# Projecting ten chunks of a second recurrence ahead of a stream of attention slots

## The chip, the core and the metric

The kernel runs on one core of one Trainium2 chip. The core has five engines with a queue of instructions each: TensorE (PE: matmuls, with weight loads as PEld), VectorE (DVE), ScalarE (ACT), GpSimd (POOL) and SyncE (SP, which issues the DMAs here). A queue is worked off in order; between engines, semaphores make one wait for another. The metric is the time of the launch in microseconds of the device, median of the runs shown, lower is better. All data is float32. In the trace each float32 matmul leaves two records, a transpose one.

## What is computed

Two batches of 4096 tokens with 256 channels go through two parts, each with a residual.

```python
x = x + attn(layernorm(x))   # a token-by-token recurrence over 4096 steps
x = x + ffn(layernorm(x))    # 2 layers of windowed attention and a gated MLP
# attn: xr, xk, xv mix each token with the one before it
r, k, v = xr @ W_r.T, xk @ W_k.T, xv @ W_v.T
# scan over tokens, for each channel:
p = max(b, k + u); out = (exp(b - p) * a + exp(k + u - p) * v) / (sum of both exps)
# ... a and b are updated; then
rwkv = sigmoid(r) * out
# group norm with mean and variance over all 4096 tokens of a batch, then @ W_o.T
# ffn, per layer: shift by a token, qkv, l2norm, rotary, 8 heads of 64,
#   attention over the own window of 128 tokens and the one before it, @ wo,
#   shift, layernorm, @ w1, a * gelu(g), @ w2
```

The group norm needs the whole batch before the first token of attention can start. So batch 0 has to finish its recurrence first; batch 1's recurrence can run beside the attention of batch 0.

## The kernel before: how it is tiled and ordered

The program is not written in the order in which it runs. Everything in `tile_block_kernel` goes through a `Plan`: each call on `nc.tensor`, `nc.vector` and so on is noted as an operation with its dependences, an estimated duration (`cost`) and a priority, the row set by `plan.at(row)` (lower goes first). `Plan.order` then places operations on the engines: on each engine, of those that can start first, the one of the lowest row. `give` emits them in that order (so nearly all instructions carry line 517). "Either" operations, mostly copies out of PSUM, go to ScalarE, or to VectorE where ScalarE is more than 700 ns (`LEAN`) later. A DMA is assumed to hold SP for 60 ns and to land 2000 ns or more after its issue. A group of matmuls into one bank, or what stands in a `piece()`, stays together.

The work, in rows:

- Rows from -101: recurrence one (`rec`, batch 0), in seven chunks of 512 tokens and two of 256. A chunk is loaded (`load`), normalized (`normed`), transposed so that channels lie on partitions (`transposed`) and projected to k, v, r (`project`, j = 1, 2, 0). Then `scans` runs the recurrence with scan instructions on VectorE and exponentials on ScalarE. Projection uses one of two ways. `split` multiplies the tokens and the shifted tokens by two scaled copies of the weights (`wnow` and `wold`): 24 matmuls of 512 columns in a chunk. `mixed` first mixes tokens and shifted tokens on VectorE (a difference `d`, then `xm` for each of k, v, r) and multiplies by the plain weights (`wraw`, which are loaded again over `wold`): half the matmuls.
- `group_norm` turns the statistics of the batch into a scale and a shift per channel.
- Slots n = 0 to 127 (rows 0 to 133, with a tail for the last blocks): one slot is one window of 128 tokens in one layer of one batch, and four slots make a block of 512 tokens. In a slot: q and k of the window are transposed (`transpose_qk`), `scores` multiplies them, `softmax` runs in four groups, `transpose_p` brings the probabilities back for `values`, and `kept`, `output` and `shift` finish the attention. Beside these, the slot projects q, k, v of the next window (`project(n + 1, j)`), squares, rotates and norms them, and runs a share of the MLP of the block before (`fill`: `gate`, `gelus`, `value`, `down`). `scores` is one piece: the values of the slot before, the last MLP rows (`down_ends`), then the eight score matmuls, in this order.
- `mixed_out` (layer 0 only) applies the group norm to a block (`z`), multiplies by W_o, adds x, stores the sum (`x1d`) and normalizes for attention; `transpose_x` transposes the block. Both take a block of 512 tokens as a whole.
- Recurrence two (`rec2`, batch 1) has 16 chunks of 256 tokens. Chunk 0 is projected ahead (row -0.5, `AHEAD` = 1), split. The scans of chunk c stand at slot 5 + int(c * 50 / 16), that is 5, 8, 11, ... up to 51, and chunk c + 1 is projected there, mixed.

```python
 for c in range(AHEAD):
        plan.at(-0.5)
        rec2.ahead(c, rec2.split)
...
            if NW + 1 + int(c * R_SLOTS / rec2.n) == n:
                plan.at(n + 0.5)
                if AHEAD <= c + 1 < rec2.n:
                    rec2.ahead(c + 1, rec2.mixed)
                rec2.scans(c)
```

Names in the profile: `arena` is the space that both recurrences share (their x, xT, k, v, r, factors and `wnow`); `bank` is any of the eight PSUM banks; `hm` holds the five 128-row parts of the MLP's hidden layer, which is free until the first block's MLP in slot 5; `kT`, `qT` are transposed keys and queries, `vr` the values shifted by a token and `dv` their difference, `pB` the probabilities for the older window, `tab` the rotary table, `h` the shifted input of the MLP, `zd` the recurrence's output in DRAM.

Of the kernel before, what the change touches and what calls it, by code (L numbers as in the profile page):

```python
# [15 lines left out]
P = 128  # L16
# [15 lines left out]
NEG = -1e38  # L32
MASKED = -3e38
R_SLOTS = 50
AHEAD = 1

ARENA = (
    (("m ls aa", 2 * T + 2, 1), ("wnow", 6 * D, 1), ("xT", 2 * T + 2, 2), ("x", 2 * T, 2), ("k v", 2 * T, 1)),
# [20 lines left out]
LEAN = 700  # L59
SLACK = 1.06  # L60
LOAD = 1283
TURN = {"row": 195, "col": 95, "full": 199}
SETS = {AF.Exp: 1, AF.Tanh: 1, AF.Gelu: 2, AF.Ln: 3}
QUADS = 4
# [2 lines left out]
class Place:  # L67


    def __init__(self, size, psum=False):  # L70
        self.size, self.psum = size, psum
        self.reads, self.writes = [], []
        self.real = None
        self.users, self.bank = set(), None
        self.turn, self.first = 0, None
# [101 lines left out]
class Plan:  # L177
# [38 lines left out]

    def dram(self, shape, name):
        place = Place(int(np.prod(shape[1:])))
        place.real = self.dram_pool.tile([P, place.size], F32, tag=name, name=name)
        return self.view(place, 0, shape)  # L220

# [75 lines left out]
    def cost(self, o):  # L297

        views = [*o.outs, *o.ins]
        n = max([v.idx.size for v in views] or [1])  # L300
        psum = any(v.place.psum for v in views)
        inside = sum(v.idx.size == n and not v.place.psum for v in o.ins)
        o.set, o.lock, o.half, o.passes, name, hold = None, False, "full", 0, o.name, None
        if o.eng == "tensor":
            trans = name == "transpose"
            left = o.args[1]
            move = o.args[2] if len(o.args) > 2 else o.args[1]
            cols = max(move.idx.size, left.idx.size) if not trans else P
            o.step = (1 if trans else 2) * (cols / 1.2 + (2 if cols >= 256 else 3))
            if not trans and left.shape[0] <= 64:  # L310
                o.half = "row"
            elif not trans and left.idx.size <= 64:
                o.half = "col"
            if o.half != "full":
                o.step /= 2
            o.time = o.step + 150
        elif o.eng == "vector":
            d = 150 + 1.04 * n
            if name == "tensor_tensor_reduce":
                d = 240 + 1.04 * n  # L320
            elif name == "tensor_tensor_scan":
                d, o.lock = 203 + 2.1 * n, True
            elif name == "scalar_tensor_tensor":
                d, o.lock = 200 + 1.05 * n, inside > 1
            elif name == "tensor_tensor":
                o.lock = inside > 1
            elif name == "tensor_scalar":
                d, o.lock = 155 + (1.27 if psum else 0.98) * n, not psum and n > 16
            elif name == "tensor_copy" and not psum:
                d, o.lock = 230 + 0.45 * n, n > 16  # L330
            elif name == "bn_aggr":
                d = 172
            elif name == "reciprocal":
                d = 147 + 4 * n
            o.step, o.time = max(d - 85, 60), d
        elif o.eng in ("scalar", "either"):
            d = (160 if psum else 195) + 0.83 * n
            if name == "scaled":
                d = 305 + 0.76 * n
            elif name == "activation":  # L340
                o.set = SETS.get(o.args[2])
                if o.args[2] == AF.Identity:
                    d = 365 + 0.87 * n
                elif isinstance(o.kw.get("bias"), View):
                    d += 85
            o.step, o.time = d - 100, d
            if "accum_out" in o.kw:
                o.time = d + 200
        elif o.eng == "gpsimd":
            o.lock = name != "memset"  # L350
            if name == "tensor_tensor":
                d = 430 + 156 * n if ALU.pow in o.args else 140 + 2.22 * n
            elif name == "tensor_scalar":
                d = 230 + 1.12 * n
            else:
                d = (100 if name == "memset" else 187) + 0.98 * n
            o.step, o.time = d, d
            hold = d if n > 64 else 100
        else:
            v = min(views, key=lambda v: v.shape[0] * v.idx.size)  # L360
            size = 4 * v.shape[0] * v.idx.size
            rows = max(v.shape[0] if v.shape[0] > 1 else v.shape[1] for v in views)
            ways = max(k for k in range(1, 17) if rows % k == 0)
            o.passes = size / 170 if ways == 16 else size / (25 * ways)
            o.step, o.time = 60, 2000 + o.passes
        o.hold = hold or o.time


    def order(self):
# [49 lines left out]
        while todo:  # L419
# [25 lines left out]
            for o in g:  # L445
# [21 lines left out]
                o.start = t  # L467
                if e == "sync":
                    dma = max(dma, t) + o.passes
                    o.end = max(t + time, dma + 2000)  # L470
                else:
                    o.end = t + time
                if o.lock and e in lock:
# [47 lines left out]
def kernel(ctx: ExitStack, tc: tile.TileContext, a: dict, out: bass.AP):  # L521
# [62 lines left out]
    class Recurrence:  # L584


        def __init__(self, b, lengths, most, spots):
            self.b, self.most, self.spots = b, most, spots
            self.turns = {}
            self.len = lengths  # L590
            self.off = [sum(lengths[:c]) for c in range(len(lengths))]
            self.n = len(lengths)
# [73 lines left out]
        def mixed(self, c, j):  # L666

            ch, tr = self.chunks[c], self.len[c]
            if "d" not in ch:
                d = ch["d"] = self.t("d", tr)  # L670
                nc.vector.tensor_tensor(d, ch["xT"][:, :, 1:], ch["xT"][:, :, :tr], ALU.subtract)
            xm = self.t("xm", tr)
            for i in range(2):
                nc.vector.scalar_tensor_tensor(
                    xm[:, i, :],
                    ch["d"][:, i, :],
                    vec[:, j, i : i + 1],
                    ch["xT"][:, i, :tr],
                    ALU.mult,
                    ALU.add,  # L680
                )
            return [(wraw, xm[:, i, :], i) for i in range(2)]
# [7 lines left out]
                for wt, off in ((wnow, 1), (wold, 0))  # L690
            ]

        def project(self, c, j, how):

            ch, tr = self.chunks[c], self.len[c]
            parts = how(c, j)
            dst = ch[j] = self.t("rkv"[j], tr)
            per = T // tr
            for o0 in range(0, 2, per):
                pm = bank([P, T])  # L700
# [13 lines left out]
                else:  # L714
                    nc.scalar.activation(to, of, AF.Tanh, scale=0.5)

        def ahead(self, c, how):
            row = plan.row
            plan.at(row - 1)
            self.load(c)  # L720
# [1 line left out]
            self.transposed(c)  # L722
            plan.at(row)
            for j in (1, 2, 0):
                self.project(c, j, how)


        def factors(self, y, c):
# [156 lines left out]
    def mixed_out(k):  # L885
# [2 lines left out]
        if l:  # L888
            return
        x, z, g = xs[k], zs[k], groups[b]  # L890
        for h in range(2):
            nc.scalar.activation(
                z[:, h, :], z[:, h, :], AF.Identity, bias=g[:, 1, h : h + 1], scale=g[:, 0, h : h + 1]
            )
        for w0 in range(0, NW, 2):
            py = bank([P, 2, D])
            for w in range(2):
                for h in range(2):
                    nc.tensor.matmul(
                        py[:, w, :],  # L900
                        z[:, h, (w0 + w) * P : (w0 + w + 1) * P],
                        wot[:, h, :],
                        start=(h == 0),
                        stop=(h == 1),
                    )
            nc.vector.tensor_tensor(x[:, w0 : w0 + 2, :], x[:, w0 : w0 + 2, :], py, ALU.add)
        nc.sync.dma_start(out=x1d[b][c], in_=x)
        for w in range(NW):
            normed(x[:, w, :])

    def normed(x):

        st = tile_of([P, 6], "st", 4)
        mv = tile_of([P, 2], "mv", 6)
        nc.vector.bn_stats(st, x)
        nc.vector.bn_aggr(mv, st)
        rs = tile_of([P, 1], "rs", 6)
        rsqrt_of(rs, mv[:, 1:2], 1, LN_EPS, ALU.add)
        nc.vector.tensor_scalar(x, x, mv[:, 0:1], rs, ALU.subtract, ALU.mult)

    def transpose_x(k):

# [4 lines left out]
            nc.gpsimd.memset(xT[:, 1, 0:1], 0.0)  # L927
        else:
            nc.gpsimd.tensor_copy(xT[:, 1, 0:1], xTs[k - 1][:, 1, T : T + 1])
        for i in range(2):  # L930
            pt = bank([P, T])
            for w in range(NW):
# [116 lines left out]
    def scores(n):  # L1049
# [6 lines left out]
        ks = slice(me, me + 1) if lone(n) else slice(me - 1, me + 1)  # L1056
        sims[n] = [bank([P, 2, 2 * W]) for _ in range(4)]
        with piece():
            if n:
                values(n - 1)  # L1060
            down_ends(n)
            for hp in range(HEADS // 2):
                for r in range(2):
# [5 lines left out]
                        start=True,  # L1069
                        stop=True,  # L1070
                    )

    def softmax(n, g):

# [255 lines left out]
        for t, n in (("pB", 1), ("h", 2), ("hT", 1), ("sq", 1), ("t2", 1), ("qk", 2), ("x", 4))  # L1330
        for i in range(n)
    ]
    lent = [(p, 0) for p in lent] + [(plan.places["hm_0"], i * 2 * T) for i in range((NM - 1) // 2)]
    spots = [{}, {}]
    for b, parts in enumerate(ARENA):
        o = 0
# [6 lines left out]
    for t in "kvrfgeq":  # L1343
        while len(spots[0].setdefault(t, [])) < 2:
            spots[0][t].insert(0, lent.pop())

    plan.at(-101)
    rec = Recurrence(0, [T] * (NB - 1) + [T // 2] * 2, T, spots[0])
# [14 lines left out]
    for j in (1, 2, 0):  # L1363
        rec.project(0, j, rec.split)
    rec2 = Recurrence(1, [TR] * (S // TR), TR, spots[1])
    for c in range(rec.n):
        if c + 1 < rec.n:
            plan.at(-90 + c)
# [8 lines left out]
        plan.hold = None  # L1377
    rec.group_norm()
    for c in range(AHEAD):
        plan.at(-0.5)  # L1380
        rec2.ahead(c, rec2.split)
    plan.at(-0.5)
    nc.sync.dma_start(out=wraw, in_=a["w_rkv"])
    rec2.start()
    plan.at(-1)
    nc.gpsimd.memset(ends, 1.0)
# [13 lines left out]
    for n in range(NN + 6):  # L1400
# [5 lines left out]
        for c in range(rec2.n):  # L1406
            if NW + 1 + int(c * R_SLOTS / rec2.n) == n:
                plan.at(n + 0.5)
                if AHEAD <= c + 1 < rec2.n:
                    rec2.ahead(c + 1, rec2.mixed)  # L1410
                rec2.scans(c)
                if c + 1 == rec2.n:
                    rec2.group_norm()
# [142 lines left out]
```

## Time and profile before

| what | value |
|---|---|
| median of 3 runs | 3010.59 us (3009.65 to 3012.26) |
| the profiled execution | 3013.12 us |
| its span on the core | 3011.2 us, 48808 instructions |
| DMA | 182.50 MB, mean 61 GB/s |
| DMAs issued by SP | 1496 |
| of the chain that ended last | PE 80%, DVE 9%, ACT 5%, DMA 2% |

Columns of the views: in the page's slices each digit is the busy share of a fortieth of the span in tenths (one slice is 75.3 us), and PEclk is the clock that TensorE was granted. A timeline row has start, length, engine, line, operation, output and inputs with shapes, the number of merged instructions, and in brackets the idle time of the engine before it with what ended it. A group row has the shape, the count, then busy us and mean ns of one, then the idle time before such instructions and who ended it. The end of a matmul is modelled, and so its start-to-start distance says more than its length.

### The profile page before, as it was taken

Reading aid. Unit: us, or ns where it says so; the run is one execution under the profiler, and the core shown is the slowest. Engines: PE = TensorE matmul, PEld = TensorE weight load, DVE = VectorE, ACT = ScalarE, POOL = GpSimd, SP = SyncE. Lnnn points to the kernel's source line nnn. Section 1 sums busy time; section 2 is a strip of 40 time slices with the busy share of each in tenths; the row PEclk is TensorE's granted clock in tenths of the full one; section 3 lists DMA queues with packets and bytes.
Section 4 is the critical chain, followed back from the end, with each engine's and each line's share of the span. In section 5 each row is a group of like instructions: output and inputs, shape, how many; then the busy total and the mean of one; then the engine's idle time right before and its main releaser. Section 6 shows DMA issues by size and latency. Waiting matters only on the chain.

```text
span 3011.2 us, 48808 instructions
## 1 busy us (share of the span) xinstructions
PE 2947.5 (98%) x15500; PEld 1912.2 (64%) x15500; DVE 2218.2 (74%) x5077; ACT 2024.9 (67%) x5378; POOL 1437.8 (48%) x1705
## 2 busy tenths in 40 slices
PE   9978999999999999999999999999999999999998
PEld 4456566666666666666666666666666666666665
DVE  7888877888788888787676766667766666667663
ACT  7877786777767777676666566656666666666663
POOL 2226655445445454555544544545444545555550
PEclk9989999999999999999999999999999999999999
DMA  2322112111112121111122221111112121111110
GB/s 83 114 74 95 40 54 64 57 56 54 61 57 69 63 63 59 51 56 53 51 63 81 85 60 59 61 61 60 46 47 75 56 63 57 55 55 54 46 43 24
DMA packets 178314, 182.50 MB, mean 61 GB/s; under 512 B 27044, under 2 KB 147716, under 8 KB 177544
## 3 DMA queue, kind: packets, MB, share of 16 engines
q1 hardware_dynamic: 178056, 179.38, 19.4%
q8 instruction: 123, 2.02, 0.3%
q14 instruction: 135, 1.11, 0.1%
HBM read 79.17 MB, written 33.55 MB: 37 GB/s over the span
## 4 chain that ended last, share of the span: by engine, by line
PE 80%; DVE 9%; ACT 5%; DMA 2%; issue 1%; SPq 1%; POOL 1%; DVEq 0%; POOLq 0%; ACTq 0%
PE bank L517 80%; DVE arena L517 3%; SPq L517 1%; ACT arena L517 1%; DMA h<-x 1%; DVE bank L517 1%; ACT pr L517 1%; ACT L517 1%; DVE nmx L517 1%; DVE sq L517 1%; ACT pr L513 1%; DVE x L517 1%; DVE rn L517 0%; DVE qk L517 0%; DVE pB L517 0%
## 5 line engine op out<-in xcount | busy, mean ns | idle before, releaser
L517 PE MATMUL bank<-wqkv,xT 128*128 128x512 f32 x1536 | 722.0, 597 | 0.4 <-ACT xT L517 0.2
L517 POOL TENSOR_TENSOR t<-qk,tab 128x256 f32<-128x256 f32 x512 | 395.3, 792 | 527.2 <-ACT qk L517 408.1
L517 PE MATMUL bank<-hT,w 128*128 128x512 f32 (+1 forms) x1408 | 644.7, 594 | 0.0
L517 ACT ACTIVATE pr<-bank,nmx 128x129 f32<-128x129 f32 (+1 forms) x1024 | 364.6, 376 | 164.8 <-DVE nmx L517 158.3
L517 PEld LDWEIGHTS bank<-hT,w 128*128 128x128 f32 (+1 forms) x1408 | 258.9, 189 | 269.0 <-issue 247.6
L517 PEld LDWEIGHTS bank<-wqkv,xT 128*128 128x128 f32 x1536 | 268.0, 191 | 229.2 <-issue 219.2
L517 POOL TENSOR_TENSOR rn<-rn,mhalf 128x16 f32<-128x16 f32 x128 | 387.8, 3030 | 8.8
L513 ACT ACTIVATE pr<-pr,sums 128x129 f32<-128x129 f32 (+1 forms) x1004 | 329.4, 413 | 42.7 <-DVE pr L517 41.3
L517 DVE TENSOR_REDUCE rn<-sq 128x16 f32<-128x1024 f32 x128 | 155.6, 1215 | 209.6 <-ACT sq L517 209.6
L517 DVE COPY_PREDICATED bank<-packs,bank 128x254 f32<-128x254 int32 x496 | 186.0, 420 | 151.1 <-PE bank L517 150.7
L517 PE MATMUL bank<-w,hm 128*128 128x256 f32 x1280 | 287.3, 379 | 0.0
L517 PEld LDWEIGHTS bank<-w,hm 128*128 128x128 f32 x1280 | 241.4, 190 | 33.2 <-issue 1.3
L517 PE MATMUL bank<-wo,oT 128*128 128x256 f32 x1024 | 250.3, 387 | 0.0
L517 PE MATMUL bank<-kT,qT 64*128 64x256 f32 (+1 forms) x2048 | 246.1, 380 | 0.0
L517 PEld LDWEIGHTS bank<-wo,oT 128*128 128x128 f32 x1024 | 187.9, 190 | 68.3 <-issue 41.0
L517 ACT COPY qk<-bank 128x512 f32<-128x512 f32 x217 | 126.8, 585 | 151.5 <-PE bank L517 143.8
L517 POOL TENSOR_TENSOR dv<-vr,vt 128x512 f32<-128x512 f32 x124 | 168.7, 1360 | 124.5 <-PE bank L517 108.7
L517 PEld LDWEIGHTS bank<-mats,pr 128*128 128x128 f32 x1148 | 134.0, 135 | 136.7 <-issue 54.0
L517 ACT ACTIVATION_READ_ACCUMULATOR pr<-bank,nmx 128x1 f32 x1024 | 218.6, 214 | 0.0
L517 DVE TENSOR_TENSOR pB<-bank,backs 128x512 f32<-128x512 f32 x248 | 169.7, 684 | 66.4 <-PE bank L517 45.6
L517 PEld LDWEIGHTS bank<-kT,qT 64*128 64x128 f32 x2048 | 190.5, 187 | 31.4 <-issue 6.5
L517 POOL TENSOR_TENSOR tab<-tab,qks 128x256 f32<-128x256 f32 x128 | 119.2, 932 | 183.3 <-DMA tab<-in_c_rot_dram 166.2
(150 smaller groups left out, 5573.8 us busy)
## 6 DMA issues: line engine op xcount, KB each, us to landing
vr<-vt SPq DMA_DIRECT2D x124, 224.0 KB
tab<-in_c_rot_dram SPq DMA_DIRECT2D x128, 128.0 KB
kT<-kT SPq DMA_DIRECT2D x64, 256.0 KB
z<-zd SPq DMA_DIRECT2D x16, 512.0 KB
x<-in_x_dram SPq DMA_DIRECT2D x16, 512.0 KB
x1d<-x SPq DMA_DIRECT2D x16, 512.0 KB
x<-x1d SPq DMA_DIRECT2D x16, 512.0 KB
h<-x SPq DMA_DIRECT2D x128, 64.0 KB
```

Of the source, the lines that this page charges most:

```text
L513: self.nc.scalar.activation(dst, src, AF.Copy, scale=scale)
L517: getattr(getattr(self.nc, o.eng), name)(*args, **kw)
```

## The change

Five edits:

1. `AHEAD` goes from 1 to 10, so chunks 0 to 9 of recurrence two are projected in one place, with their loads at row 3 and their projections at row 4. `SPLIT` = 3 of them are split, the others mixed, with the weights loaded again between (row -0.5). `INSIDE` = 2 of them leave k, v, r in the arena. The eight others put them into one of three `far` buffers, from which SP stores them to DRAM (`away`); `back` loads them at the slot where they were projected before. Early chunks have a `d` and an `xm` buffer of their own. These five buffers lie in `hm`. In exchange recurrence one no longer borrows space in `hm`, and the turns of xT, x, k, v, r start at the other buffer.
2. For block 0 alone, `mixed_out` and `transpose_x` go by 128 tokens: z, W_o, sum and normalization of each 128 tokens stand by themselves, the normalized tokens go into another x tile, and each 128 tokens have a transpose bank and an eviction of their own.
3. The planner's costs: a DMA holds SP for 370 ns (580 or 800 for one between two SBUF tiles, by how it divides) instead of 60, and it lands after 2500 ns (`LAND`) instead of 2000.
4. In `scores`, the values of the slot before come after the score matmuls instead of ahead of them.
5. `normed` can write to another tile than it reads.

```diff
-AHEAD = 1
+AHEAD = 10
+SPLIT = 3
+INSIDE = 2
...
+            inner = len(views) == 2 and not any(v.place.outer for v in views)
+            o.step = 370 if not inner else 580 if ways in (1, 16) else 800
+            o.time = LAND + o.passes
...
             for j in (1, 2, 0):
-                self.project(c, j, how)
+                self.project(c, j, how, ("far", "far", "far") if away else "rkv")
+                if away:
+                    d = self.away[c, j] = plan.dram([P, 2, self.len[c]], f"away_{c}_{j}")
+                    nc.sync.dma_start(out=d, in_=self.chunks[c][j])
+
+        def back(self, c):
+            for j in (1, 2, 0):
+                dst = self.chunks[c][j] = self.t("rkv"[j], self.len[c])
+                nc.sync.dma_start(out=dst, in_=self.away[c, j])
...
+        if k == 0:
+            xs[k] = tile_of([P, NW, D], "x", 4)
+        for w0 in range(0, NW, 1 if k == 0 else 2):
+            ws = range(w0, w0 + (1 if k == 0 else 2))
+            if k == 0 or w0 == 0:
+                cols = slice(w0 * P, (w0 + 1) * P if k == 0 else T)
...
+            if k == 0:
+                normed(xs[k][:, w0, :], x[:, w0, :])
...
+        if k == 0:
+            for w in range(NW):
+                pt = bank([P, 2, P])
+                for i in range(2):
+                    nc.tensor.transpose(pt[:, i, :], x[:, w, i * P : (i + 1) * P], ident)
+                either(xT[:, :, 1 + w * P : 1 + (w + 1) * P], pt)
+            return
...
         with piece():
-            if n:
-                values(n - 1)
             down_ends(n)
...
+            if n:
+                values(n - 1)
...
+    spare = [(plan.places["hm_0"], i * 2 * TR) for i in range(NM - 1)]
+    spots[1].update(earlyd=spare[:1], earlyxm=spare[1:2], far=spare[2:])
...
     for c in range(AHEAD):
-        plan.at(-0.5)
-        rec2.ahead(c, rec2.split)
+        if c == SPLIT:
+            plan.at(-0.5)
+            nc.sync.dma_start(out=wraw, in_=a["w_rkv"])
+        plan.at(4)
+        rec2.chunks[c]["early"] = True
+        rec2.ahead(c, rec2.split if c < SPLIT else rec2.mixed, c >= INSIDE)
...
                 if AHEAD <= c + 1 < rec2.n:
                     rec2.ahead(c + 1, rec2.mixed)
+                elif INSIDE <= c + 1 < AHEAD:
+                    rec2.back(c + 1)
                 rec2.scans(c)
```

More of the change, by code (lines that the diff above doesn't have):

```diff
@@ L61 @@
 LOAD = 1283
+LAND = 2500
 TURN = {"row": 195, "col": 95, "full": 199}
@@ L72, in __init__ @@
         self.reads, self.writes = [], []
+        self.outer = False
         self.real = None
@@ L218, in dram @@
         place = Place(int(np.prod(shape[1:])))
+        place.outer = True
         place.real = self.dram_pool.tile([P, place.size], F32, tag=name, name=name)
@@ L364, in cost @@
             o.passes = size / 170 if ways == 16 else size / (25 * ways)
-            o.step, o.time = 60, 2000 + o.passes
+            inner = len(views) == 2 and not any(v.place.outer for v in views)
+            o.step = 370 if not inner else 580 if ways in (1, 16) else 800
+            o.time = LAND + o.passes
         o.hold = hold or o.time
@@ L469, in order @@
                     dma = max(dma, t) + o.passes
-                    o.end = max(t + time, dma + 2000)
+                    o.end = max(t + time, dma + LAND)
                 else:
@@ L588, in __init__ @@
             self.b, self.most, self.spots = b, most, spots
-            self.turns = {}
+            self.turns, self.away = {}, {}
             self.len = lengths
@@ L668, in mixed @@
             ch, tr = self.chunks[c], self.len[c]
+            early = "early" if ch.get("early") else ""
             if "d" not in ch:
-                d = ch["d"] = self.t("d", tr)
+                d = ch["d"] = self.t(early + "d", tr)
                 nc.vector.tensor_tensor(d, ch["xT"][:, :, 1:], ch["xT"][:, :, :tr], ALU.subtract)
-            xm = self.t("xm", tr)
+            xm = self.t(early + "xm", tr)
             for i in range(2):
@@ L691, in split, with project @@
             ]
-        def project(self, c, j, how):
+        def project(self, c, j, how, put="rkv"):
             ch, tr = self.chunks[c], self.len[c]
             parts = how(c, j)
-            dst = ch[j] = self.t("rkv"[j], tr)
+            dst = ch[j] = self.t(put[j], tr)
             per = T // tr
@@ L715, in project, with ahead @@
                     nc.scalar.activation(to, of, AF.Tanh, scale=0.5)
-        def ahead(self, c, how):
+        def ahead(self, c, how, away=False):
             row = plan.row
@@ L890, in mixed_out @@
         x, z, g = xs[k], zs[k], groups[b]
[L891 to L897, printed above, removed]
+        if k == 0:
[4 more added lines that the diff above has]
+                cols = slice(w0 * P, (w0 + 1) * P if k == 0 else T)
+                for h in range(2):
+                    nc.scalar.activation(
+                        z[:, h, cols],
+                        z[:, h, cols],
+                        AF.Identity,
+                        bias=g[:, 1, h : h + 1],
+                        scale=g[:, 0, h : h + 1],
+                    )
+            py = bank([P, len(ws), D])
+            for w in ws:
                 for h in range(2):
                     nc.tensor.matmul(
-                        py[:, w, :],
-                        z[:, h, (w0 + w) * P : (w0 + w + 1) * P],
+                        py[:, w - w0, :],
+                        z[:, h, w * P : (w + 1) * P],
                         wot[:, h, :],
@@ L905, in mixed_out, with normed @@
                     )
-            nc.vector.tensor_tensor(x[:, w0 : w0 + 2, :], x[:, w0 : w0 + 2, :], py, ALU.add)
+            x1 = x[:, w0 : w0 + len(ws), :]
+            nc.vector.tensor_tensor(x1, x1, py, ALU.add)
+            if k == 0:
+                normed(xs[k][:, w0, :], x[:, w0, :])
         nc.sync.dma_start(out=x1d[b][c], in_=x)
-        for w in range(NW):
-            normed(x[:, w, :])
-    def normed(x):
+        if k:
+            for w in range(NW):
+                normed(x[:, w, :])
+    def normed(dst, x=None):
+        x = dst if x is None else x
         st = tile_of([P, 6], "st", 4)
@@ L918, in normed @@
         rsqrt_of(rs, mv[:, 1:2], 1, LN_EPS, ALU.add)
-        nc.vector.tensor_scalar(x, x, mv[:, 0:1], rs, ALU.subtract, ALU.mult)
+        nc.vector.tensor_scalar(dst, x, mv[:, 0:1], rs, ALU.subtract, ALU.mult)
     def transpose_x(k):
@@ L929, in transpose_x @@
             nc.gpsimd.tensor_copy(xT[:, 1, 0:1], xTs[k - 1][:, 1, T : T + 1])
+        if k == 0:
+            for w in range(NW):
+                pt = bank([P, 2, P])
[3 more added lines that the diff above has]
+            return
         for i in range(2):
@@ L1332 @@
     ]
-    lent = [(p, 0) for p in lent] + [(plan.places["hm_0"], i * 2 * T) for i in range((NM - 1) // 2)]
+    lent = [(p, 0) for p in lent]
     spots = [{}, {}]
@@ L1365 @@
     rec2 = Recurrence(1, [TR] * (S // TR), TR, spots[1])
+    rec2.turns = dict.fromkeys(("xT", "x", "k", "v", "r"), 0)
     for c in range(rec.n):
@@ L1379 @@
     for c in range(AHEAD):
-        plan.at(-0.5)
-        rec2.ahead(c, rec2.split)
+        if c == SPLIT:
[4 more added lines that the diff above has]
+        rec2.ahead(c, rec2.split if c < SPLIT else rec2.mixed, c >= INSIDE)
     plan.at(-0.5)
-    nc.sync.dma_start(out=wraw, in_=a["w_rkv"])
+    if AHEAD <= SPLIT:
+        nc.sync.dma_start(out=wraw, in_=a["w_rkv"])
     rec2.start()
```

## The prediction, made before the changed kernel ran

> **What bounds the kernel now.** I read the page first: which engine is full, and where it is not.
>
> ```profile
> PE 2947.5 (98%) x15500; PEld 1912.2 (64%) x15500; DVE 2218.2 (74%) x5077; ACT 2024.9 (67%) x5378; POOL 1437.8 (48%) x1705
> ...
> PE   9978999999999999999999999999999999999998
> ...
> PEclk9989999999999999999999999999999999999999
> ```
>
> TensorE is busy for 98% of the span. Only slices 3 and 4 (150 to 300 us) and the last one show less. So time can come from two places: matmuls that go away, or idle TensorE time in those slices. Next, the windows, cut where a stage begins (the timeline gives the first score matmul of slots 0, 7, 10, 36, 48 and 127 at 260.0, 381.2, 439.0, 1041.4, 1309.8 and 2946.4 us); the columns are length, then PE, PEld, DVE, ACT and POOL busy, clock, DMA share, GB/s.
>
> ```profile
> 150.00:216.00 66.00, 50.34 (x192) 36.90 (x191) 54.41 (x106) 46.42 (x77) 13.73 (x27) 0.92 0.20 67
> 216.00:260.00 44.00, 39.88 (x151) 27.95 (x149) 39.39 (x96) 31.04 (x49) 21.84 (x33) 0.92 0.39 131
> 260.00:381.00 121.00, 110.25 (x645) 70.88 (x646) 99.46 (x242) 91.58 (x266) 80.84 (x97) 0.99 0.16 48
> ...
> 439.00:1041.00 602.00, 594.54 (x3191) 393.79 (x3189) 490.43 (x1110) 427.04 (x1121) 299.74 (x353) 1.00 0.20 59
> 1041.00:1310.00 269.00, 261.97 (x1432) 173.53 (x1430) 223.17 (x486) 194.80 (x515) 139.42 (x162) 0.99 0.19 57
> ```
>
> The first three rows hold most of the idle time, and VectorE is at 82 to 90% in them. Busy time flatters TensorE (overlapping ends, matmuls at a lowered clock: 0.92), so I count its **own work**. In the undisturbed timeline a matmul record starts 429 ns after one of 512 columns, 215 after 256, 109 after 128; a pair on half the array takes one such time, and each change between full, row-split and column-split use adds 93 ns. Counts by these intervals give 2882 us of work, 129 us idle. By stage, in us (DVE and ACT: counts by each group's mean, less the overlap of 66 and 49 ns that the whole trace shows per instruction):
>
> start to slot 0: time 260.0, PE 217.9, idle 42.1; DVE 221
> slots 0 to 7: time 121.2, PE 104.1, idle 17.1; DVE 101, ACT 98
> 7 to 10: time 57.8, PE 56.5, idle 1.3; DVE 44
> 10 to 36: time 602.4, PE 583.2, idle 19.2; DVE 496
> 36 to 48: time 268.4, PE 254.4, idle 14.0; DVE 219
> 48 to 127: time 1636.6, PE 1612.8, idle 23.8
> 127 to end: time 64.8, PE 53.1, idle 11.7
>
> Why slot 0 is late: the timeline of TensorE, then of ScalarE.
>
> ```profile
> 215.63 0.38 PE L517 MATMUL bank<-gmv,mats 128*128 128x2 f32 x2 [4.20 <-DVE gmv L517]
> ...
> 221.83 4.14 PE L517 MATMUL bank<-wot,z 128*128 128x256 f32 x16
> ...
> 238.28 10.57 PE L517 MATMUL bank<-wqkv,xT 128*128 128x512 f32 x24 [0.24 <-ACT xT L517]
> ...
> 260.02 1.16 PE L517 MATMUL bank<-kT,qT 64*128 64x128 f32 x16
> ```
>
> ```profile
> 220.35 1.52 ACT L517 ACTIVATE z<-z,group 128x512 f32<-128x512 f32 x2
> ...
> 237.64 1.07 ACT L517 COPY xT<-bank 128x512 f32<-128x512 f32 x2 [5.62 <-PE bank L517]
> ```
>
> The scale arrives at 220.35; the first projection starts 18 us later, since the block passes each step as a whole.
>
> **The change, part by part.** I count the same way on the changed kernel's instruction order.
>
> *Projections ahead.* A mixed chunk is 24 records of 215 ns and 4 transposes of 109: 5.6 us of TensorE. A split chunk has 48 records: 10.8. Chunk 0 was early and split already; chunks 1 and 2 become split (adds 2 x 5.15 = **10.3 us** of work, 2892.3 in all), 3 to 9 are moved only (39.2). The new order has all of them between the last projections of recurrence one and slot 6, which are the idle slices. On VectorE a mixed chunk costs a subtraction (0.75) and six multiply-adds (mean 0.50): 3.75 us, so the two split ones save 7.5. The new sums: start to 0: PE 226.9, DVE 200; 0 to 7: PE 138.7, DVE **142.4**, ACT 124; 7 to 10: PE 59.9, DVE 57; 10 to 36: PE 536.0, DVE 451; 36 to 48: PE 264.7, DVE 221; then 1612.9 and 53.2 for TensorE. About 21 us of VectorE work (first scans of recurrence two) also leave the stretch before slot 0 and come back behind it.
>
> *First block by 128 tokens.* The columns of w=0 now go alone: two z steps (about 0.4 each; 0.59 is the row at 256 columns), 4 records of 215, an add (0.41), statistics (0.6), the power on POOL (about 0.9), normalization (0.4), two transposes, an eviction. From 220.35 that is about 5.5 us: first projection at about 226 instead of 238.3. ScalarE issues all eight z steps and three other instructions (1.6 us) ahead of that eviction, which also ends near 225.5. TensorE's order then has 19 us of work up to the scores: not before 245. The rotation chain took 21.7 us before, with 4 us in VectorE's queue. I take slot 0 at **248** (245 to 256: early evictions and normalizations stand between the last scans): idle 21 instead of 42.
>
> *Slots 0 to 7.* Three engines are now nearly full. In slots 5 to 7 of before (41.2 us; PE 38.0, DVE 36.2, ACT 38.1) the busiest reached 92.5%; in slots 0 to 3 (46.7 us; DVE 36.5) VectorE reached 78%. I take the first, since it is the mix of work nearest to the new one: 142.4 / 0.925 = **154 us**, idle 15.3. The ends are 147 (97%, TensorE's share in 10 to 36) and 182 (78%).
>
> *Later stages.* 7 to 10: 59.9 + 1.4. 10 to 36: the ratio of VectorE to TensorE work stays (0.85, now 0.84), so idle time falls with the length: 17. 36 to 48: 12, since part of the 14 is a stall on late transfers, which the planner now assumes to land 500 ns later. From 48 on, as before.
>
> *Scores before values.* The built order has 392 changes of array use in both kernels, at 93 ns, with the same pairs to drain: nothing. Two windows shrink. In the steady slots at least 3.9 us of matmuls lay from the q/k transposes to the scores, now 2.57; the evictions end 1.71 to 1.78 us after the first transpose when ScalarE takes them undelayed. From the values to the output projection, where values' bank must be evicted, at least 1.97; the eviction ends 0.905 after the last values matmul. Both fit, so I cost it at nothing; that cover is 0.8 us, and each us beyond it would cost 1 us in a slot, 128 us in all slots. Where VectorE evicts (up to 5.6 us late) the order has put more work between. Softmax starts some 1.9 us sooner, which only an unfilled slot can use.
>
> *Round trip through DRAM and issue times.* 24 stores and 24 loads, 256 KB each, are added: SP issues cost 0.32 to 0.97 us, so 15 to 47 us on a queue that mostly waits. A store waits for an eviction (SP waits for a bank 3.9 us on average, 21.8 at most); behind it stand vr, kT, h and the mask row for pB, and POOL and the values wait for these. Nearest row: TensorE lost 5.5 us to that pB row in the whole run. I take 0, bounds -5 (fewer VectorE waits for h, 68 us in the waits) to +10.
>
> GpSimd shares its SBUF interfaces with VectorE, and instructions with two SBUF inputs contend: the Trainium skill, "GPSIMD Engine Reference", section Key points. That speaks against moving multiply-adds under the rotations of slots 0 to 7. The trace agrees in direction:
>
> ```profile
> L517 POOL TENSOR_TENSOR t<-qk,tab 128x256 f32<-128x256 f32 x46 | 36.6, 821 | 16.3 <-ACT qk L517 15.8 <-DVE sums L517 0.4
> ```
>
> That is from 240 to 440 us; from 2000 to 2900 us the mean is 748. By the rule alone 28 rotations would lose perhaps 2 us (an estimate from these rows); without it the sum stays.
>
> **Sum.** 248 + 154 + 61.3 + 553.0 + 276.7 + 1636.7 + 64.9 = 2994.6 us span, 16.6 below 3011.2. The profiled execution took 3013.1, 1.9 more than its span, and the median is 2.5 below it: **2994** for the median.
>
> **Rivals.** (1) *VectorE becomes the bound, slower.* Place: slots 0 to 7. If its share stays at the 78 to 80% of slots 0 to 3, the stretch takes 178 to 182 us: 24 to 28 more, so 3018 to 3022. From 171 us on (VectorE under 83%) the gain is gone, from 177 us on (81%) the kernel is slower. For it: one xm buffer, three far buffers, in-order queues that also wait for SP. Against it: slots 5 to 7, and no early chunk is on the slots' own chain. (2) *No change.* Slot 0 at 252 and the stretch at 160 to 168 us eat the gain: 3004 to 3012; the 10.3 us of added matmuls help it. (3) *More than forecast.* Slot 0 at 245, the stretch at 147, and 10 less idle between 10 and 48, because VectorE has 45 us less there: 2974. That the projections are not early is excluded by the order.
>
> **Chances.** Forecast (2980 to 3004) 0.50; rival 3 0.12; rival 2 (3004.6 to 3016.6) 0.18; rival 1 0.20. A measurement of this kernel tells 0.2%, 6 us, from no change. So faster 0.62, same 0.18, slower 0.20. Range 2970 to 3022: it takes in all three rivals' sums.
>
> **What would show it.** First projection of slot 0 near 226 and its scores near 248; slots 0 to 7 in 150 to 160 us with VectorE over 90%; a clock near 1.00 from 150 to 300 us; slot 10 near 463 (24 late), slot 36 near 1016 (25 early), and steady slots of the same length. Wrong, if slot 10 comes after 475, if PE waits for qT or oT in steady slots, or if the gating of block 0 (slot 5 on), which needs hm back from the early chunks, stalls TensorE.

## The result, and the profile after

The changed kernel takes **2972.08 us** (median of 4 runs, 2970.99 to 2973.21) against 3010.4 before: a ratio of 0.987 (0.986 to 0.989), 38 us less. The profiled span fell from 3011.2 to 2969.2 us. The forecast was 2994: the right sign, inside the range, and less than half of the gain.

The page of the changed kernel, engines, slices and clock as before:

```profile
PE 2945.0 (99%) x15548; PEld 1913.7 (64%) x15548; DVE 2250.9 (76%) x5088; ACT 2018.8 (68%) x5359; POOL 1449.3 (49%) x1705
...
PE   9999999999999999999999999999999999999998
...
PEclk9999999999999999999999999999999999999999
```

The two dips of slices 3 and 4 are gone, and so is the low digit of the clock. The windows, cut at the changed kernel's own slots (0 at 244.1, 7 at 392.0, 10 at 452.9, 36 at 998.5, 48 at 1267.3 us):

```profile
150.00:216.00 66.00, 64.96 (x284) 50.90 (x282) 58.48 (x120) 52.75 (x90) 16.77 (x34) 1.00 0.22 72
216.00:244.00 28.00, 26.98 (x105) 17.57 (x105) 22.07 (x48) 20.46 (x37) 15.98 (x24) 1.00 0.53 183
244.00:392.00 148.00, 145.48 (x799) 103.08 (x798) 138.81 (x338) 115.97 (x308) 90.37 (x117) 0.98 0.32 105
453.00:998.00 545.00, 543.45 (x2969) 354.52 (x2969) 455.10 (x1024) 399.63 (x1071) 282.36 (x333) 1.00 0.22 66
998.00:1267.00 269.00, 268.23 (x1461) 178.63 (x1460) 220.00 (x481) 197.37 (x516) 134.47 (x158) 1.00 0.20 60
```

From 150 to 216 us TensorE is busy for 64.96 us where it was 50.34, and the clock is full. In slots 0 to 7 VectorE is busy for 94% and TensorE for 98%: both at once. But the last two rows matter as much: 1.5 and 0.8 us without a matmul, where the kernel before had 7.5 and 7.0. Most of that part was not in the forecast, which took idle time between slots 10 and 48 from 33.2 to 29 us.

The start of slot 0, on TensorE and ScalarE:

```profile
212.13 0.28 PE L524 MATMUL bank<-gmv,mats 128*128 128x2 f32 x2
...
219.92 3.62 PE L524 MATMUL bank<-wot,z 128*128 128x256 f32 x16
...
224.87 1.98 PE L524 MATMUL bank<-wqkv,xT 128*128 128x512 f32 x4 [0.46 <-ACT xT L524]
...
244.15 1.16 PE L524 MATMUL bank<-kT,qT 64*128 64x128 f32 x16
```

```profile
218.66 3.19 ACT L524 ACTIVATE z<-z,group 128x128 f32<-128x128 f32 x8
224.44 0.37 ACT L524 COPY xT<-bank 128x256 f32<-128x256 f32 x1 [0.93 <-PE bank L524]
```

The first projection is at 224.9 (forecast 226), 6.2 us after the scale arrived (18 before). The group norm itself is 3.5 us earlier, although early matmuls stand right up to it.

The same count as in the prediction (time less TensorE's own work, by stage, in us) is the measure in all that follows. PE work is 2882.0 us in kernels with one chunk ahead or with SPLIT 1, else 2892.3.

| kernel | start to 0 | 0 to 7 | 7 to 10 | 10 to 48 | 48 to 127 | tail | idle in all |
|---|---|---|---|---|---|---|---|
| before | 42.1 | 17.1 | 1.3 | 33.2 | 23.7 | 11.8 | 129.2 |
| forecast | 21 | 15.3 | 1.4 | 29 | 23.8 | 11.7 | 102.3 |
| changed | 17.2 | 9.2 | 0.9 | 13.8 | 24.5 | 11.3 | 76.9 |
| x1 no ahead | 36.4 | 8.7 | 1.6 | 15.7 | 24.9 | 11.6 | 98.9 |
| x2 old DMA costs | 21.7 | 10.0 | 1.6 | 18.8 | 27.3 | 11.7 | 91.1 |
| x3 values first | 18.4 | 10.4 | 1.3 | 16.6 | 19.8 | 11.8 | 78.3 |
| x4 whole block | 22.5 | 6.6 | 1.7 | 12.4 | 24.7 | 12.9 | 80.8 |
| y1 scores only | 43.8 | 10.4 | 0.8 | 21.5 | 24.4 | 10.8 | 111.7 |
| y2 DMA costs only | 37.5 | 16.0 | 2.8 | 17.5 | 20.7 | 11.6 | 106.1 |
| y3 scores and DMA | 38.4 | 10.0 | 3.4 | 15.0 | 24.1 | 12.4 | 103.3 |
| y4 control 1.07 | 42.9 | 14.6 | 1.1 | 26.6 | 28.3 | 11.3 | 124.8 |
| w1 issue time only | 43.8 | 18.7 | 2.6 | 20.8 | 20.6 | 12.1 | 118.6 |
| w2 landing only | 37.1 | 13.6 | 0.7 | 24.6 | 19.8 | 12.5 | 108.3 |
| w3 control 1.05 | 44.0 | 13.8 | 4.0 | 28.4 | 29.9 | 12.2 | 132.3 |
| z1 SPLIT 1 | 30.1 | 8.2 | 1.8 | 14.0 | 24.4 | 11.4 | 89.9 |
| z2 scores first to slot 51 | 17.6 | 9.2 | 0.9 | 13.9 | 20.9 | 11.3 | 73.8 |
| z4 six ahead | 16.0 | 8.9 | 3.2 | 14.5 | 24.4 | 11.7 | 78.7 |

### The profile page after: what moved, and what is told of

It is laid out like the page before. It is cut to its first block, busy times and chain, and to the rows that moved or that the text cites. A ratio compares the mean times of both kernels' runs of the same rounds, so it can differ in the third digit from the quotient of the medians.

```text
span 2969.2 us, 48964 instructions
## 1 busy us (share of the span) xinstructions
PE 2945.0 (99%) x15548; PEld 1913.7 (64%) x15548; DVE 2250.9 (76%) x5088; ACT 2018.8 (68%) x5359; POOL 1449.3 (49%) x1705
## 3 DMA queue, kind: packets, MB, share of 16 engines
q1 hardware_dynamic: 184968, 191.96, 20.9%
## 4 chain that ended last, share of the span: by engine, by line
PE 92%; DVE 3%; ACT 3%; issue 1%; POOL 0%; DMA 0%; SPq 0%; POOLq 0%; ACTq 0%; DVEq 0%
PE bank L524 92%; ACT pr L524 1%; ACT L524 1%; DVE arena L524 1%; DVE bank L524 0%; ACT pr L520 0%; DVE sq L524 0%; DVE qk L524 0%; DVE h L524 0%; DVE nmx L524 0%; DVE hm L524 0%; DVE pB L524 0%; ACT arena L524 0%; ACT oT L524 0%; ACT hm L524 0%
## 5 line engine op out<-in xcount | busy, mean ns | idle before, releaser
L524 PE MATMUL bank<-hT,w 128*128 128x512 f32 (+1 forms) x1408 | 652.2, 595 | 0.0
L524 POOL TENSOR_TENSOR t<-qk,tab 128x256 f32<-128x256 f32 x512 | 383.6, 768 | 471.2 <-ACT qk L524 362.3
L524 PE MATMUL bank<-w,hm 128*128 128x256 f32 x1280 | 294.0, 381 | 0.0
L524 ACT COPY qk<-bank 128x512 f32<-128x512 f32 x225 | 132.3, 588 | 170.5 <-PE bank L524 164.0
L524 PE MATMUL bank<-wo,oT 128*128 128x256 f32 x1024 | 243.0, 380 | 1.4 <-ACT oT L524 1.3
L524 ACT COPY hm<-bank 128x512 f32<-128x512 f32 x170 | 99.8, 587 | 174.1 <-PE bank L524 173.1
L524 PE MATMUL bank<-pT,vt 128*64 128x128 f32 x2048 | 203.3, 279 | 0.0
```

Source lines behind the costliest of these rows:

```text
L524: getattr(getattr(self.nc, o.eng), name)(*args, **kw)
```

## The experiments

Fifteen runs. Ratios are against the kernel before, run on the same chip beside them. Its own median moved between 3010.4 and 3012.8 us from one set of runs to the next, so a difference of 2 or 3 us between kernels of different sets is not clear of noise. The idle times by stage are of one execution each.

### One edit taken out of the change

**x1**, one chunk ahead: `AHEAD = 1`.

> The changed kernel with AHEAD back at 1 (one chunk ahead, eight transfers to DRAM and back gone), all other edits kept. Theory A (the early projections carry the gain): the idle time of TensorE returns up to slot 10, the 10.3 us of added matmuls go: about 2995 us. Theory B (planner costs or the order in the slots carry most of it): at most 2980 us. By either, idle between slots 10 and 48 tells more: if it stays near 14 us, lighter load on VectorE was not what removed the 19 us there.

Measured 2983.5 us, 0.990 (0.989 to 0.992). Without the early chunks the kernel is still 29 us faster than the kernel before beside it (3012.6), of a gain of 38 in all. The early chunks are worth 11.4 us by the medians, and 11.7 by the profiled spans: 22.0 us of idle time less the 10.3 of added matmuls. Between slots 10 and 48 the idle time stays low without them (15.7). The time lies between theories A and B, nearer to B.

**x2**, the planner's old DMA costs:

```diff
-            inner = len(views) == 2 and not any(v.place.outer for v in views)
-            o.step = 370 if not inner else 580 if ways in (1, 16) else 800
-            o.time = LAND + o.passes
+            o.step, o.time = 60, LAND + o.passes   # and LAND = 2000
```

> The changed kernel with the planner's old DMA costs (60 ns on SP, landing after 2000 ns), all other edits kept. Theory D (late transfers caused the stalls between slots 10 and 48, the new costs removed them): idle there rises from 14 to about 28 us, time about 2986 us. Theory S (the order in the slots removed them): within 4 us of the changed kernel, 2968 to 2976 us.

Measured 2984.7 us, 0.991 (0.989 to 0.992): as theory D has it in time (12.6 us), not in place. Only 5 of the 14.2 us of idle time come back between slots 10 and 48; 4.5 come before slot 0 and 2.8 after slot 48.

**x3**, values first again (the `values(n - 1)` of `scores` moved back ahead of `down_ends`):

> The changed kernel with the values of the last slot ahead of the scores again, all other edits kept. My prediction's step (costs and brings nothing): 2968 to 2976 us, same waits. Theory S (scores sooner, so the softmax no longer makes the transposes of the probabilities wait): idle between slots 10 and 48 rises by about 8 us (the waits for softmax that the kernel before shows there), some more in slots 0 to 7: about 2983 us.

Measured 2971.6 us, 0.986 (0.985 to 0.988): no difference, as the prediction's step said, and theory S fell for the whole change. The stages say more: 5.6 us more idle time before slot 48, and 4.7 us less from there to slot 127.

**x4**, the first block as a whole:

> The changed kernel with the first block handled as a whole again, all other edits kept. My prediction's step: slot 0 starts about 12 us later (256 instead of 244 us); early projections fill part of that gap, so 4 to 12 us slower: 2976 to 2984 us. Rival (the gap is filled by early matmuls either way): within 3 us of the changed kernel.

Measured 2975.3 us, 0.988 (0.986 to 0.989). Slot 0 starts at 260.2 instead of 244.1, but 10.8 us more of matmuls stand ahead of it. Splitting the block is worth about 3 us here, hardly clear of noise, because the early chunks fill the same gap.

### One edit added to the kernel before

Since taking out any one edit gave little idle time back between slots 10 and 48, I put single edits into the kernel before, with a control.

**y1**, only the order in `scores`:

> The kernel before with one edit: scores ahead of the values of the last slot. Idle of TensorE between slots 10 and 48 was 33.2 us before and 13.8 after the whole change; taking out either the early chunks (15.7), the DMA costs (18.8) or the order in the slots (16.6) gave little of it back. Theory R (several edits each remove the same stalls): this one alone brings that idle to about 18 us, time 2994 to 3000 us. Theory C (the kernel before holds an unlucky order, which any small move of the plan dissolves): the same here, and in the control. Theory N (only a pair of edits does it): it stays near 30 us, 3006 to 3014 us.

Measured 2996.0 us, 0.995 (0.993 to 0.996). **y2**, only the DMA costs:

> The kernel before with one edit: the planner's new DMA costs. Theory R: idle between slots 10 and 48 falls from 33 to 15 to 20 us, and from slot 0 to 10 from 18 to about 12, time 2984 to 2998 us. Theory N: 3006 to 3014 us.

Measured 2991.3 us, 0.993 (0.992 to 0.995). Between slots 10 and 48 the idle time is in the range that theory R gave (17.5); from slot 0 to 10 it did not fall (18.8 against 18.4). **y3**, both:

> The kernel before with two edits: scores first and the new DMA costs, nothing else. It differs from the changed kernel without early chunks (2983.5 us) by the first block in parts and the borrowed space. Theory R: about 2984 to 2992 us, idle between slots 10 and 48 near 16 us. If the first block or the borrowed space did it: over 3000 us.

Measured 2987.4 us, 0.992 (0.990 to 0.994). **y4** and **w3**, `SLACK = 1.07` and `1.05`:

> A control: the kernel before with a neutral number of the planner moved (durations of the three other engines scaled by 1.07 instead of 1.06), which shifts the order a little and means nothing else. It measures how far the time moves by an order's luck. Theory C: idle between slots 10 and 48 falls well below 33 us and the time moves by over 10 us. Theories R and N: within about 6 us of the kernel before, 3004 to 3017 us.

> A second control: the planner's neutral factor at 1.05 instead of 1.06. If luck of the order is small beside the effects above: within 6 us of the kernel before, 3005 to 3017 us.

Measured 3009.4 us, 0.999 (0.998 to 1.000), and 3012.0 us, 1.000 (0.999 to 1.001). A small move of the plan moves a stage by up to 7 us but the whole by 2 or so. The 15.7 us by scores first and the 20.4 by the DMA costs are far more than these two moves brought, so I take them for effects and not for luck of the order: theory R. Together (24.3) they are much less than their sum.

Which stalls, the waits tell (who waits, for whom; total us, times, longest). First the whole run, before:

```profile
DVE st L517 <- DMA h<-x: 68.0, 52, 2.9
PEld bank L517 <- ACT pr L513: 51.6, 146, 2.7
...
PE bank L517 <- ACT pr L513: 9.7, 20, 2.5
```

With scores first alone (y1):

```profile
DVE st L517 <- DMA h<-x: 55.0, 64, 2.5
...
PEld bank L517 <- ACT oT L517: 23.7, 61, 1.9
PEld bank L517 <- ACT pr L513: 23.7, 84, 0.4
```

With the DMA costs alone (y2):

```profile
PEld bank L522 <- ACT pr L518: 42.2, 142, 0.9
...
DVE st L522 <- DMA h<-x: 14.8, 18, 2.5
```

Scores first starts the softmax sooner, so the transposes of the probabilities wait for it half as long and at most 0.4 us. In exchange the output projection now waits for oT (23.7 us of its weight loads; none such stood in the list before). With the DMA costs, most of VectorE's waits for h are gone. The same list for slots 10 to 48 alone, before:

```profile
PEld bank L517 <- ACT pr L513: 22.5, 51, 1.7
DVE st L517 <- DMA h<-x: 18.1, 13, 2.6
PEld bank L517 <- DVE qk L517: 9.2, 8, 3.4
PE bank L517 <- DVE qk L517: 5.9, 3, 3.0
```

The stalls for qk are common to both edits: the 9.2 us of weight loads are 2.5 in y1, 4.3 in y2 and 2.2 in y3, while the controls keep 8.5 (y4) and 10.4 (w3). The wait for pr falls with scores first (5.2 in y1, 4.2 in y3); with the DMA costs alone it is 15.7, hardly below the controls (22.8 and 17.5). Where the rest of the overlap of the two edits lies was not located. The longest of the stalls for qk (3.0 in the last row), in the kernel before, at 1228 to 1239 us, read on SP, VectorE and TensorE:

```profile
1228.12 1.80 SPq L517 DMA_DIRECT2D h<-x  x3
1230.02 0.54 SPq L517 DMA_DIRECT2D tab<-in_c_rot_dram  x1
1230.61 1.46 SPq L517 DMA_DIRECT2D vr<-vt  x2
1232.11 0.82 SPq L517 DMA_DIRECT2D h<-x  x1
```

```profile
1234.94 0.43 DVE L517 BATCH_NORM_STATS2 st<-h 128x6 f32<-128x256 f32 x1 [2.12 <-DMA h<-x]
...
1237.54 1.22 DVE L517 TENSOR_TENSOR qk<-sq,rn 128x1024 f32<-128x1024 f32 x1
```

```profile
1238.82 1.09 PE L517 MATMUL bank<-mats,qk 128*128 128x128 f32 x8 [2.99 <-DVE qk L517]
```

The last of four h transfers is issued 4 us after the first. The plan, which counted 60 ns for each issue, had put the statistics of h ahead of the last step of q and k on VectorE. VectorE waits 2.12 us in order, q and k are late, and TensorE stands for 2.99 us.

Two more runs take the halves of the DMA costs apart. **w1**, issue times only; **w2**, landing after 2500 ns only:

> The kernel before with half of the new DMA costs: an issue holds SP for 370 to 800 ns, landing still assumed after 2000 ns. Theory I (the queue's issue times were what the plan had wrong: the last of four h transfers is issued 4 us after the first in the trace of before, 0.2 us by 60 ns each): most of the 20 us, 2990 to 2996 us, and the waits of VectorE's statistics for h fall from 68 us to under 30. Theory L (the landing): little, 3003 to 3010 us.

> The kernel before with the other half: 60 ns per issue, landing assumed after 2500 ns. Theory I: little, 3003 to 3010 us, waits for h above 45 us. Theory L: 2990 to 2996 us.

Measured 3002.7 us, 0.997 (0.996 to 0.998), and 2992.5 us, 0.994 (0.992 to 0.995). My theory I fell, though its mechanism is there: with the issue times the waits for h drop to 17.5 us in the whole run and the idle time between slots 10 and 48 to 20.8, but the stages up to slot 10 get 4.6 us worse. The later landing brings twice the gain with 37.3 us of those waits left in the whole run. Between slots 10 and 48 the halves leave almost the same of the 18.1 us: 6.6 (w1) and 6.9 (w2); with both, 2.2 are left (y2). So the total of a wait over the whole run does not tell what it costs: y3, faster than y2, has 38.2 us of it where y2 has 14.8. The later landing helps from the start on (37.1 and 13.6 us in the first two stages; the second is hardly more than what the controls moved). It is not a truer number: in the 59 cases before where VectorE's statistics waited over 200 ns, the median from the start of the last h issue to their start is 2.10 us. Why the margin helps where it does was not taken apart further, and stays open.

### What limits the early stretch, and a faster version

**z1**, `SPLIT = 1`:

> The changed kernel with SPLIT 1: chunks 1 and 2 are mixed on VectorE instead of split, so TensorE has 10.3 us less and VectorE 7.5 us more, all of it before slot 7. Theory V (my prediction: VectorE is what slots 0 to 7 wait for): no faster than the changed kernel, 2970 to 2978 us. Theory P (TensorE is the bound even there, since it was 94% busy with its own work in that stretch): 8 to 10 us faster, 2962 to 2965 us.

Measured 2974.7 us, 0.988 (0.986 to 0.989), no faster, as theory V said, but for another reason. Slots 0 to 7 are as full as in the changed kernel (idle 8.2). The loss is ahead of slot 0: the mixed chunks need plain weights and `xm`, which come too late. TensorE in z1, and its window:

```profile
200.91 3.75 PE L524 MATMUL bank<-hm,wold 128*128 128x256 f32 x8 [3.96 <-DMA wold<-in_w_rkv_dram]
209.77 1.22 PE L524 MATMUL bank<-hm,wold 128*128 128x256 f32 x2 [5.11 <-DVE hm L524]
```

```profile
150.00:216.00 66.00, 56.24 (x222) 41.59 (x221) 57.78 (x119) 52.41 (x89) 16.13 (x30) 0.90 0.24 76
```

Split chunks cost twice the matmuls, but they need nothing but xT and the weights that are there.

**z4**, `AHEAD = 6`:

> The changed kernel with six chunks ahead instead of ten. Ten ahead save 22 us of idle time against one ahead, all but 2 us of it before slot 7, and add 10.3 us of matmuls, which six ahead add as well. Theory G (the idle time to be filled ends early, so six are enough): within 3 us of the changed kernel, 2969 to 2975 us. Rival (each chunk moved saves its 2 us): 2980 us.

Measured 2974.6 us, 0.988 (0.986 to 0.989): theory G. The last four of the ten chunks are worth 2.5 us here, which is not clear of noise.

**z2** keeps scores first up to slot 51 and takes values first from there, as x3's stages suggest; **z3** adds `SPLIT = 1`:

```diff
         with piece():
+            if n >= 52:
+                values(n - 1)
             down_ends(n)
...
-            if n:
+            if 0 < n < 52:
                 values(n - 1)
```

> The changed kernel with scores ahead of values up to slot 51 and values first from slot 52 on. With values first, slots 48 to 127 had 19.8 us idle instead of 24.5, and slots 0 to 48 had more idle time (28.3 against 23.9). If both halves keep what they had: about 4 us faster, 2968 us. If the difference in the late slots is luck of the order: 2970 to 2974 us.

> Both of the last two edits together. If they add up: 2958 to 2962 us by theory P, 2966 to 2974 by theory V.

Measured 2967.0 us (2966.1 to 2967.8), 0.985 (0.984 to 0.987), and 2970.5 us, 0.986 (0.985 to 0.988). z2 is the fastest kernel here, about 5 us below the changed one, whose runs (2971.0 to 2973.2) are of another set; both halves kept what they had. In its own set, z3 is 4.2 us below z1 by the late order, and 3.5 above z2 by `SPLIT = 1`, with no overlap of the runs: the split chunks pay, and theory P fell again.

## Why the prediction was right in sign and half in size

By its own steps, span 2994.6 forecast and 2969.2 measured, 25.4 us less:

- **Projections ahead: right.** The added matmuls were 10.3 us, the idle slices were filled, slot 10 came 13.9 us later than before (forecast 24) and slot 36 42.9 earlier (forecast 25). Taking the edit out loses 11.4 us net (x1).
- **First block by 128 tokens: right in mechanism.** First projection at 224.9 instead of 226, slot 0 at 244.1 instead of 248 (-3.9 us). x4 shows what the stage sum hid: with early chunks beside it, it is worth only some 3 us.
- **Slots 0 to 7: mis-sized** (147.9 us, forecast 154). I took the busiest engine to 92.5%; by the same count VectorE reached 142.3 / 147.9 = 96% (its busy time in the trace is 94%), near the good end of 147. The order in the slots can have a part in it: alone, it takes the idle time there from 17.1 to 10.4 us (y1).
- **"Scores before values" at nothing, and "round trip through DRAM and issue times" at 0 (bounds -5 to +10): these are the steps that failed.** Alone in the kernel before they bring 15.7 and 20.4 us, together 24.3. Taken out of the whole change, the DMA costs lose 12.6 us and the order in the slots nothing: each does a part of what the other does. I costed the order by its own matmuls and windows, and left aside that the transposes of the probabilities wait for the softmax (51.6 us of weight loads before, 23.7 in y1). I costed the DMA constants by the transfers that they describe, with 2 us for late ones in slots 36 to 48, and not by what the plan does with them. The round trip itself was rightly put at 0: its 48 issues take SP 0.32 to 0.62 us each, 19.6 in all, and no wait for these transfers of 0.2 us or more stands in the changed kernel's list.
- **Later stages: wrong for that reason.** I read the idle time of slots 10 to 48 as a share that follows VectorE's load (17 + 12 us). It was 13.8, and 15.7 with the load unchanged (x1). Either of the two edits alone brings the 33.2 us before down to 21.5 (y1) or 17.5 (y2), both to 15.0 (y3), the controls to 26.6 and 28.4. 15.3 of the 25.4 us are here.
- **The parts that were priced came out as a sum.** Added in one order, by profiled spans, the two edits above take 25.9 us (y3 against before), the first block by 128 tokens with its moved space 4.4 (x1 against y3) and the early chunks 11.7 (changed against x1). The last two make 16.1, where the forecast had 16.6 for everything. That these agree so well is partly luck: stages are off both ways in it, and another order of adding would share the gain out differently.
- **Steady slots: right as a sum.** 24.5 us idle, 23.8 forecast, by luck of two errors that cancel. Kernels with new DMA costs, whole or half, have 19.8 to 20.9 us there with values first (x3, y2, w1, w2, z2), and those with both edits have 24.1 to 24.9. The controls move this stage by up to 6 us, but the two groups lie apart, and z2 and z3 gain 4 to 5 us by the late order: scores first does cost some 4 us here. The prediction's sign of being wrong, waits for oT in steady slots, came true for the weight loads: 39 waits between slots 48 and 127, 11.0 us, none before. The window from the values to the output projection, which it took to fit, did not always.

Of the rivals, the third had the right place (10 to 48, slot 0 at 245, 147 us in slots 0 to 7) and 2974 us, but gave lighter load as its cause, which x1 contradicts: its number is luck. The rotation rows on GpSimd, read there as agreeing with contention (means of 821 and 748 ns), have the same median in both windows, 727 ns; a few long ones, up to 1.78 us, make the means, so these rows do not show it.

## What to carry to other kernels

In a kernel whose order a planner makes, a constant of the planner is a part of the schedule: cost such an edit by the waits of in-order engines for what the constant describes, stage by stage, and not by their total over the run; even so, the margin for landing (w2) brought twice what the truer issue times (w1) brought, and why stays open. Two edits that each remove the same stalls can look worthless when taken out one at a time and add up badly; take each out and put each in alone, with a control that only jogs the order. When work is moved into a gap, ask what it still has to wait for there: the form that costs more but needs less can be the better filler.

## What was not expected of the hardware

- After 3.96 us without work, eight records of 256 columns took 3.75 us in z1; eight such take 1.89 in the changed kernel, and the granted clock of the window was 0.90. An idle TensorE paid twice there. After 2.99 us without work, in the stall shown above, eight records of 128 columns took 1.09 us, as long as eight in the changed kernel with no wait ahead of them (at 241.41 us). The Trainium skill, "TensorE: Matmul & The Clock Gate", Part 1, says that an idle window of about 3.4 us halves the clock; these rows agree.
- In the same 148 us (slots 0 to 7 of the changed kernel) VectorE was busy for 94%, and TensorE had 94% of the time filled by its own counted work.
